# A graph attention kernel with a quantile layer: the first search's transposes one by one, and larger pieces in the quantile sort

## The chip, the cores and the metric

The kernel runs on one core of a Trainium2 chip. The time is the device time of one launch in microseconds. Before the change the median of three runs is 3615.5 us (3614.76 to 3617.49).

## The reference

Two graph layers run one after the other on 4096 nodes of 128 features, with a random adjacency matrix of 0s and 1s (about 32 neighbours a node).

```python
# layer 0: attention over the neighbours, 8 heads
Wh = einsum('nd,hde->hne', nodes, W)
f1 = einsum('hnd,hd->hn', Wh, a1);  f2 = einsum('hnd,hd->hn', Wh, a2)
e = leaky_relu(f1[:, :, None] + f2[:, None, :], 0.2)
att = softmax(where(adj > 0, e, -9e15), axis=-1)
h = elu(einsum('hnm,hmd->hnd', att, Wh))
x1 = layernorm(nodes + elu(concat_heads(h) @ W1 + b1)) * gamma + beta

# layer 1: per feature, three quantiles over the kept neighbours
m = where(num_nbr > 5, ceil(num_nbr / 2), 1)
keep = mask & ~((rank_in_list + 1) % m == 0)
svals = sort(where(keep, x1, big), axis=neighbours)
agg = mean of svals at the places of the 0.25, 0.5 and 0.75 quantile
s = 0.5 * agg + 0.5 * x1
out = s @ W.T + b + x1
```

## The kernel before

The nodes form 32 tiles of 128. The work has four stages.

**First search.** For each node the columns of its neighbours are listed. ScalarE turns half a row tile of the adjacency matrix (128 x 2048 integers) into signs (`sgn`, L642). TensorE multiplies them into keys of 512 columns (two matmuls into the PSUM tile `key`, L681 and L684; `key` has two buffers). VectorE takes the eight largest of each 128 columns (L648), and from those, eight at a time, the list (L653, L655). One step of the generator `neighbours` is one such round: keys of 512 columns for one tile, and one further eight of the list of the tile before. Eight rounds are a tile. After every third tile of the first block, `complete_records` makes the records, in three further steps.

The first block has six tiles, hence 7 x 8 + 2 x 3 = 62 steps. After each of them but the first, the loop at L324 takes one step of the generator `node_rows`. That generator loads W, the attention vectors, the last layer's weights (`wl_sb`) and the node features (`rec`) on ScalarE's DMA queue, folds W and the vectors into `wa` on VectorE, transposes the 32 node tiles on TensorE, copies them out of PSUM on ScalarE (`xT`), multiplies them by `wa`, copies the products (`F`) and stores the rows, features and attention terms, to `xt_d` in HBM on SyncE's queue (L592). In the version before, four transposes make one step and the four products of the previous four another.

**Attention.** The nodes are ranked by their number of neighbours and their records scattered to HBM (GpSimd). Then in blocks of 6, 10 and 16 tiles the neighbours' rows are gathered from `xt_d`, one row for each of 128 partitions a gather (L219), and weighed. The search of the next block runs in between, on VectorE and TensorE.

**Lists of layer 1.** They are made at the end of the last block, with the weights `wt` of the quantile places.

**Quantiles.** Nodes are sorted by length of list. They are handled in 21 units of one tile or of two: unit 0, then the single tiles 24 to 31, then the pairs (22,23) down to (2,3), then tile 1. For a unit of k tiles with n kept neighbours at most, GpSimd gathers n x k rows of `x1` into `vals` (two buffers) and the nodes' own rows into `xs`. VectorE runs a selection network over the n slots, whose steps are elementwise minima and maxima of slots (L1225, between `vals`, two `work` tiles and `goal`). TensorE and ScalarE weigh the results (`st_ps`, L1244), apply the last layer, and GpSimd scatters `o` to the output (L228). GpSimd's queue holds the rows of the next unit ahead of the scatter of the unit before, then the rows of the unit after that. A new unit's `vals` takes the buffer of the unit two before it.

The network's work is issued in pieces: a minimum or maximum of slots that lie at regular distances is one instruction, of c x m x 128 x k columns. The kernel counts how long VectorE has been running since the last turn (`then`, in us, from the constants `TT_FIX`, `TT_EACH`, `TT_OVER`). After more than `TURN_MIN` us it puts in a turn, a copy of one PSUM column (`junk` from `still`, L1196)[...]. A piece that would run beyond `TURN_MAX` is cut so that it ends near `TURN_AIM`.

The order of instructions on TensorE, VectorE, ScalarE and GpSimd is that of the program (`manual_schedule`).

Of the kernel before, what the change touches and what calls it, by code (L numbers as in the profile page):

```python
# [9 lines left out]
F32 = mybir.dt.float32  # L10
# [9 lines left out]
P = 128  # L20
N = 4096
D = 128
H = 8
NT = N // P
# [61 lines left out]


TT_FIX, TT_EACH, TT_OVER = 0.148, 0.001042, 0.077
TURN_MIN, TURN_AIM, TURN_MAX = 1.25, 1.45, 1.7


R_NUM, R_OWN, R_F1 = L, L + 1, L + 2
# [1 line left out]
R_X = R_F1 + H  # L94
# [148 lines left out]
def kernel(  # L243
# [61 lines left out]
    with tc.tile_pool(name="setup", bufs=1) as sp, tc.tile_pool(  # L305
# [15 lines left out]
        )  # L321
        iota(nc, rowi, [[1, P]])
        rows = node_rows(tc, sp, pp, rec, x, W, W_sb, a1, a2, Wl, wa, WlT, ident, bad, xt_d)
        for i, _ in enumerate(search(0, BLOCKS[0])):  # L324
            if i > 0:
# [216 lines left out]
def node_rows(tc, sp, pp, rec, x, W, W_sb, a1, a2, Wl, wa, WlT, ident, bad, xt_d):  # L542


    nc = tc.nc
    c = NT // 4
    load = nc.scalar.dma_start
    load(W_sb, W.rearrange("h d e -> d h e"))
    yield
    a_b = sp.tile([P, 2, H * D], F32, name="a_b")  # L550
    for i, a in enumerate((a1, a2)):
        load(a_b[:, i, :], a.rearrange("h d -> (h d)").partition_broadcast(P))
    wl_sb = sp.tile([P, D], F32, name="wl_sb")
    load(wl_sb, Wl)
    yield
    for i in range(4):
        for _ in range(3):
            yield
        load(
            rec[:, ts(i, c), R_X : R_X + D],  # L560
            x[ts(i, c * P), :].rearrange("(t p) d -> p t d", p=P),
        )
    for i in range(2):
        wprod = sp.tile([P, H, D], F32, name="wprod")
        nc.vector.tensor_tensor(
            wprod, W_sb, a_b[:, i, :].rearrange("p (h d) -> p h d", h=H), ALU.mult
        )
        nc.vector.tensor_reduce(wa[:, ts(i, H)], wprod, AX.X, ALU.add)
        yield
    F = sp.tile([P, NT, 2 * H], F32, name="F")  # L570
    xT = f_ps = None
    for t in range(0, NT + 8, 4):
        if f_ps is not None:
            nc.scalar.copy(F[:, t - 8 : t - 4, :], f_ps)
            f_ps = None
        if xT is not None:
            f_ps = pp.tile([P, 4, 2 * H], F32, name="f_ps")
            for u in range(4):
                nc.tensor.matmul(f_ps[:, u, :], lhsT=xT[:, ts(u, P)], rhs=wa, start=True, stop=True)
            xT = None  # L580
        yield
        if t < NT:
            xt_ps = pp.tile([P, 4 * P], F32, name="xt_ps")
            for u in range(4):
                nc.tensor.transpose(xt_ps[:, ts(u, P)], rec[:, t + u, R_X : R_X + D], ident)
            xT = sp.tile([P, 4 * P], F32, name="xT", bufs=2)
            nc.scalar.copy(xT, xt_ps)
        yield
    for dst, src in ((R_F1, F[:, :, 0:H]), (R_X + D, F[:, :, H:])):
        nc.vector.tensor_scalar(rec[:, :, dst : dst + H], src, FMAX, -FMAX, ALU.min, ALU.max)  # L590
    for i in range(4):
        nc.sync.dma_start(  # L592
            xt_d[ts(i, c * P), :].rearrange("(t p) w -> p t w", p=P),
            rec[:, ts(i, c), R_X:],
        )
    pad = sp.tile([P, XW], F32, name="pad")
    nc.gpsimd.memset(pad[:, 0:D], 0.0)
    nc.gpsimd.memset(pad[:, D:], PADF)
    nc.sync.dma_start(xt_d[N:, :], pad)
    yield  # L600
    sq = sp.tile([P, NT, 2 * H], F32, name="sq")
    nc.vector.tensor_tensor(sq, F, F, ALU.mult)
    fm = sp.tile([P, NT], F32, name="fm")
    nc.vector.tensor_reduce(fm, sq, AX.X, ALU.max)

    nc.vector.tensor_scalar(fm, fm, FMAX * FMAX, None, ALU.is_le)
    nc.vector.tensor_scalar(bad[:, 3, :], fm, -1.0, 1.0, ALU.mult, ALU.add)
    yield
    wl_ps = pp.tile([P, 4 * P], F32, name="xt_ps")[:, 0:D]
    nc.tensor.transpose(wl_ps, wl_sb, ident)  # L610
    nc.scalar.copy(WlT, wl_ps)
# [886 lines left out]
```

## Time and profile before

| | |
|---|---|
| median of three runs | 3615.5 us |
| the profiled execution's own time | 3611.84 us |
| its span, first to last instruction | 3610.1 us |
| first search, first keys to the last list | 8 to 116 us |
| first gather of rows for the attention | 150.8 us |
| first sorting piece of the quantile stage | 1857.3 us |
| last sorting piece | 3596.6 us |
| turns | 1295, 148 ns each |
| sorting pieces | 2649 |

The largest groups of the quantile stage (line, engine, operation, tiles, shapes and count, then busy us and mean ns, then idle time before them):

```profile
L1225 DVE TENSOR_TENSOR work<-work 128x512 f32<-128x512 f32 x507 | 335.9, 682 | 0.1
L1225 DVE TENSOR_TENSOR work<-work 128x1024 f32<-128x1024 f32 x273 | 334.2, 1229 | 0.0
L1196 DVE COPY junk<-still 128x1 f32<-128x1 f32 x1270 | 187.5, 148 | 0.0
L219 POOL DMA_INDIRECT vals<-x_d,idx x970 | 998.3, 1029 | 315.4 <-issue 281.9 <-DVE junk L1196 20.2 <-DMA vals<-x_d,idx 10.4
```

Durations overlap: an instruction of VectorE begins some 0.08 us before the one ahead of it ends, so costs on the engine are read from starts. DVE is VectorE, PE TensorE, ACT ScalarE, POOL GpSimd and SP SyncE. The window of these groups begins at 1900 us, so some counts are below the total.

### The profile page before, as it was taken

The page shows a single profiled execution, that of the slowest core. Times are in us where ns is not written, and L with a number is a line of the kernel's source. Part 1 is how long each engine was busy: PE and PEld are TensorE (multiplying, and loading weights), DVE is VectorE, ACT ScalarE, POOL GpSimd, SP SyncE. Part 2 cuts the span into 40 slices and gives each one's busy share as a digit, 9 for nine tenths or more (in the row PEclk, how much of TensorE's full clock was granted, in tenths as well). Part 3 has the DMA queues.
Part 4 walks back from the last instruction along what each step waited for, and adds up shares of the span by engine and source line. Part 5 has one row for each costly group of instructions (what it writes and reads, how often), then busy time and mean ns, then how long its engine had stood idle before and what let it go on. Part 6 is the DMA issues. An engine that isn't in the chain of part 4 may idle for free. (4 is left out here: it accounts for less than half of the span.)

```text
span 3610.1 us, 22900 instructions
## 1 busy us (share of the span) xinstructions
PE 1258.1 (35%) x5323; PEld 951.4 (26%) x5323; DVE 2742.8 (76%) x7591; ACT 399.5 (11%) x555; POOL 2344.3 (65%) x2341
## 2 busy tenths in 40 slices
PE   6377667878456454456610000000000000001101
PEld 3044545445455454355510000000000000000101
DVE  7787548877345122157448999999999999999998
ACT  3122122322111011111110000000000000000000
POOL 1375767757777777777557776777555766667530
PEclk9965557566556555555555555555555555555555
DMA  6443244432222222222111111111111111111100
GB/s 212 132 147 90 67 149 139 142 123 70 59 63 55 55 55 54 66 58 55 43 38 48 48 47 41 46 47 46 39 34 37 47 44 40 43 45 47 38 20 3
DMA packets 109137, 237.46 MB, mean 66 GB/s; under 512 B 46720, under 2 KB 63104, under 8 KB 100800
## 3 DMA queue, kind: packets, MB, share of 16 engines
q0 software_dynamic: 74368, 156.34, 15.5%
q10 hardware_dynamic: 14848, 70.85, 5.7%
q1 hardware_dynamic: 19776, 8.73, 1.1%
q8 instruction: 44, 0.72, 0.1%
q14 instruction: 101, 0.83, 0.1%
HBM read 224.60 MB, written 11.15 MB: 65 GB/s over the span
## 5 line engine op out<-in xcount | busy, mean ns | idle before, releaser
L219 POOL DMA_INDIRECT G<-xt_d,idx x1124 | 1096.6, 976 | 416.3 <-issue 324.0
L219 POOL DMA_INDIRECT vals<-x_d,idx x1024 | 1052.3, 1028 | 333.9 <-issue 298.0
L1225 DVE TENSOR_TENSOR work<-work 128x512 f32<-128x512 f32 (+6 forms) x1405 | 959.4, 710 | 0.4
L1244 PE MATMUL st_ps<-dg,goal 128*128 128x128 f32 x286 | 71.8, 429 | 1644.7 <-DVE goal L1225 1574.6
L1225 DVE TENSOR_TENSOR work<-work,work 128x512 f32<-128x512 f32 (+5 forms) x958 | 604.9, 655 | 0.7
L1244 PEld LDWEIGHTS st_ps<-dg,goal 128*128 128x128 f32 x286 | 63.8, 324 | 1651.0 <-issue 1650.2
L1012 PE MATMUL y<-wide,G 128*128 128x32 f32 (+3 forms) x2248 | 482.7, 392 | 26.9 <-DVE wide L999 26.9
L1012 PEld LDWEIGHTS y<-wide,G 128*128 128x128 f32 x2248 | 461.2, 309 | 62.3 <-DVE wide L999 30.0
L648 DVE MAX8 first<-key 128x8 f32<-128x128 f32 x1024 | 225.2, 281 | 119.0 <-PE key L684 118.5
L949 DVE TENSOR_TENSOR z<-G,f1x 128x128 f32<-128x128 f32 (+5 forms) x92 | 29.0, 328 | 307.9 <-DMA G<-xt_d,idx 302.7
L228 POOL DMA_INDIRECT out_dram<-o,own_i x32 | 51.0, 1593 | 295.3 <-ACT o L1270 276.1
L681 PE MATMUL key<-sgn,markb 128*128 128x512 bf16 x256 | 149.3, 583 | 145.3 <-DVE first L648 98.2
L1196 DVE COPY junk<-still 128x1 f32<-128x1 f32 x1295 | 191.2, 148 | 0.0
L1225 DVE TENSOR_TENSOR work<-vals 128x1024 f32<-128x1024 f32 (+8 forms) x140 | 138.8, 1007 | 46.2 <-DMA vals<-x_d,idx 45.9
L642 ACT ACTIVATE sgn<-adj_t 128x2048 bf16<-128x2048 int32 x64 | 122.1, 1907 | 355.4 <-PE key L681 304.8
L1043 PE MATMUL small<-W_sb,late 128*128 128x128 f32 x512 | 126.0, 430 | 88.4 <-DVE late L1040 88.4
L1243 ACT ACTIVATE dg<-ident,wt 128x128 f32<-128x128 f32 x143 | 47.5, 393 | 955.9 <-PE st_ps L1244 955.6
L964 PE MATMUL small<-z,own 128*4 128x32 f32 (+6 forms) x438 | 49.6, 280 | 284.8 <-ACT z L956 284.8
L684 PE MATMUL key<-parts,oneb 64*128 64x512 bf16 x256 | 147.2, 575 | 0.2 <-POOL parts L237 0.2
L1043 PEld LDWEIGHTS small<-W_sb,late 128*128 128x128 f32 x512 | 111.7, 324 | 102.7 <-DVE late L1040 99.0
L980 PE MATMUL rz<-rden,ownT 4*128 4x32 f32 (+6 forms) x438 | 97.8, 386 | 78.0 <-DVE rden L975 63.0
L1031 PE MATMUL hT<-late,W_sb 128*128 128x128 f32 x512 | 110.9, 385 | 35.4 <-ACT late L1025 35.4
(184 smaller groups left out, 1763.3 us busy)
## 6 DMA issues: line engine op xcount, KB each, us to landing
adj_t<-in_adj_dram ACTq DMA_DIRECT2D x64, 1024.0 KB
G<-xt_d,idx POOLq DMA_INDIRECT x1124
vals<-x_d,idx POOLq DMA_INDIRECT x1024
R<-rec_d SPq DMA_DIRECT2D x128, 26.2 KB
xt_d<-rec SPq DMA_DIRECT2D x4, 544.0 KB
rec<-in_x_dram ACTq DMA_DIRECT2D x4, 512.0 KB
narrow<-rec_d SPq DMA_DIRECT2D x68, 5.2 KB
a_b<-in_L_gnn_a_dram ACTq DMA_DIRECT2D x2, 512.0 KB
```

Source lines behind the costliest of these rows:

```text
L219: nc.gpsimd.indirect_dma_start(out=dst, out_offset=None, in_=rows, in_offset=bass.IndirectOffsetOnAxis(ap=idx, axis=0),)
L642: nc.scalar.activation(sgn, adj_t, AF.Sign, accum_out=cnt[:, i : i + 1])
L648: nc.vector.max(first[:, ts(c0 // CW + c, 8)], key[:, ts(c, CW)])
L681: nc.tensor.matmul(key, lhsT=markb, rhs=sgn[:, ts(b, 512)], start=True, stop=False)
L684: nc.tensor.matmul(key, lhsT=oneb[0:64, :], rhs=parts[1][:, ts(r - 1, 512)] if r else parts[0], start=False, stop=True)
L980: nc.tensor.matmul(rz[:, layer[i] * H : (layer[i] + w - g0) * H], lhsT=ownT[w][:, r, :], rhs=rden.rearrange("p (g r h) -> p r g h", r=k // ...
L1012: nc.tensor.matmul(yf[:, ts(g, c)], lhsT=G[:, col + j - a, 0:D], rhs=pf[:, ts(j, c)], start=(i == 0 and g % (w // 2) == w // 2 - 1), stop= ...
L1031: nc.tensor.matmul(hT[:, ts(h, P)], lhsT=consts["W_sb"][:, h, :], rhs=yT[:, h, :], start=True, stop=True)
L1043: nc.tensor.matmul(o, lhsT=hv[:, h, :], rhs=consts["W1_sb"][:, h, :], start=(h == 0), stop=(h == H - 1))
L1196: nc.vector.tensor_copy(junk, late["still"])
L1225: nc.vector.tensor_tensor(slots_of(dst, (j, c, s, m), size), slots_of(a, (i, c, s, m), size), slots_of(b, (i + d, c, s, m), size), op,)
L1244: nc.tensor.matmul(st_ps[:, u, :], lhsT=goal[:, (j * k + u) * D : (j * k + u + 1) * D], rhs=dg, start=(j == 0), stop=False,)
```

## The change

Three things are changed.

1. The quantile stage's limits: a turn after more than 1.1 us (before 1.25), pieces cut to end near 1.9 us (before 1.45), and only if they would run beyond 2.4 us (before 1.7). A piece of 2048 columns stays whole.
2. In `node_rows`, one transpose and one product go behind each round, the product three tiles behind its transpose; the copy `xT` is of one tile, in five buffers, and each four products are copied to `F` one step after the last of them.
3. The loads of W, the vectors and the last layer's weights start four rounds later and the next two further on; the node features follow two rounds apart instead of three.

```diff
-TURN_MIN, TURN_AIM, TURN_MAX = 1.25, 1.45, 1.7
+TURN_MIN, TURN_AIM, TURN_MAX = 1.1, 1.9, 2.4
...
     load = nc.scalar.dma_start
+    for _ in range(4):
+        yield
     load(W_sb, W.rearrange("h d e -> d h e"))
-    yield
+    for _ in range(2):
+        yield
     a_b = sp.tile([P, 2, H * D], F32, name="a_b")
...
     for i in range(4):
-        for _ in range(3):
+        for _ in range(2):
             yield
...
-    xT = f_ps = None
-    for t in range(0, NT + 8, 4):
-        if f_ps is not None:
-            nc.scalar.copy(F[:, t - 8 : t - 4, :], f_ps)
-            f_ps = None
-        if xT is not None:
-            f_ps = pp.tile([P, 4, 2 * H], F32, name="f_ps")
-            for u in range(4):
-                nc.tensor.matmul(f_ps[:, u, :], lhsT=xT[:, ts(u, P)], rhs=wa, start=True, stop=True)
-            xT = None
+
+    LAG = 3
+    turned, f_ps = [], None
+    for t in range(NT + LAG):
+        if t < NT:
+            xt_ps = pp.tile([P, 4 * P], F32, name="xt_ps")[:, 0:P]
+            nc.tensor.transpose(xt_ps, rec[:, t, R_X : R_X + D], ident)
+            xT = sp.tile([P, P], F32, name="xT", bufs=LAG + 2)
+            nc.scalar.copy(xT, xt_ps)
+            turned.append(xT)
+        u = t - LAG
+        if u >= 0:
+            if u % 4 == 0:
+                f_ps = pp.tile([P, 4, 2 * H], F32, name="f_ps")
+            nc.tensor.matmul(f_ps[:, u % 4, :], lhsT=turned.pop(0), rhs=wa, start=True, stop=True)
         yield
-        if t < NT:
-            xt_ps = pp.tile([P, 4 * P], F32, name="xt_ps")
-            for u in range(4):
-                nc.tensor.transpose(xt_ps[:, ts(u, P)], rec[:, t + u, R_X : R_X + D], ident)
-            xT = sp.tile([P, 4 * P], F32, name="xT", bufs=2)
-            nc.scalar.copy(xT, xt_ps)
-        yield
+        if u > 0 and u % 4 == 3:
+            nc.scalar.copy(F[:, u - 3 : u + 1, :], f_ps)
```

## The prediction

> **What bounds the kernel now.** I read the page first (busy shares, slices), then busy time by stretch, then the timelines of single engines where a stretch was not clear.
>
> ```profile
> PE 1258.1 (35%) x5323; PEld 951.4 (26%) x5323; DVE 2742.8 (76%) x7591; ACT 399.5 (11%) x555; POOL 2344.3 (65%) x2341
> DVE  7787548877345122157448999999999999999998
> POOL 1375767757777777777557776777555766667530
> L228 POOL DMA_INDIRECT out_dram<-o,own_i x32 | 51.0, 1593 | 295.3 <-ACT o L1270 276.1
> ```
>
> No engine bounds the whole span. From slice 21 on VectorE is at 9 in every slice, while GpSimd, which issues the gathers, sits 276 us waiting for the result `o` of a unit whose sort has not ended. So the quantile stage is VectorE's. Before it, GpSimd stands at 7 tenths over long stretches, and that is full: a gather takes 0.94 us, and the next begins 0.30 us after it.
>
> ```profile
> 24.67:44.00 19.33, 11.15 (x20) 1.95 (x19) 18.95 (x69) 5.70 (x6) 0.83 (x3) 1.00 1.05 354
> 44.00:80.00 36.00, 35.27 (x123) 22.22 (x123) 27.27 (x118) 12.79 (x22) 0.00 (x0) 1.00 0.27 88
> 1857.30:3596.60 1739.30, 122.00 (x528) 104.84 (x529) 1723.92 (x3944) 56.56 (x177) 1114.61 (x1064) 0.52 0.14 40
> ```
>
> The columns are window, length, then busy time and count of PE, weight loads, DVE, ACT, POOL. The quantile stage is 1739.3 us long and VectorE idles 15 us of it (13.9 at its start, where the second unit's gathers are awaited). In the first search VectorE is full from 24.67 to 44 and then, with the transposes, loses 36.00 - 27.27 = 8.7 us to a TensorE that is full.
>
> ```profile
> 50.81 1.89 PE L579 MATMUL f_ps<-wa,xT 128*128 128x16 f32 x8
> 52.53 0.59 PE L681 MATMUL key<-sgn,markb 128*128 128x512 bf16 x1
> 53.59 1.12 PE L585 MATMUL xt_ps<-ident,rec 128*128 128x128 f32 x4
> 54.50 0.63 PE L681 MATMUL key<-sgn,markb 128*128 128x512 bf16 x1
> 53.70 0.89 DVE L648 MAX8 first<-key 128x8 f32<-128x128 f32 x4 [1.14 <-PE key L684]
> 24.67 0.89 DVE L648 MAX8 first<-key 128x8 f32<-128x128 f32 x4 [4.81 <-PE key L684]
> 150.82 0.98 POOL L219 DMA_INDIRECT G<-xt_d,idx  x1 [5.63 <-issue]
> ```
>
> Starts give the cost in the queue: four products 1.72 us (50.81 to 52.53), two key products 1.06, four transposes 0.91.
>
> ```profile
> 2109.24 0.95 DVE L1225 TENSOR_TENSOR work<-work,vals 128x768 f32<-128x768 f32 x1
> 2110.11 0.15 DVE L1196 COPY junk<-still 128x1 f32<-128x1 f32 x1
> 2110.18 1.48 DVE L1225 TENSOR_TENSOR work<-vals 128x1280 f32<-128x1280 f32 x1
> 2111.57 0.15 DVE L1196 COPY junk<-still 128x1 f32<-128x1 f32 x1
> 2109.43 1.57 POOL L219 DMA_INDIRECT vals<-x_d,idx  x1 [0.30 <-issue]
> 2111.31 1.17 POOL L219 DMA_INDIRECT vals<-x_d,idx  x1 [0.30 <-issue]
> ```
>
> This is the rule of the stage. The gather begun at 2109.43 ends at 2111.00, 0.89 after the turn at 2110.11; that of 2111.31 ends at 2112.48, 0.91 after the turn at 2111.57. A gather waits for the next start of a VectorE instruction and ends 0.90 later. By the timeline it is let in between two sorting pieces too, with no turn between (about 90 of 100 such cases). A turn costs VectorE 0.069 us (2110.11 to 2110.18), not its 0.15.
>
> [...] Here, from starts, a piece of n columns takes 0.0685 + n/960 us (512: 0.602; 1024: 1.135), so the fixed part is 0.0685.
>
> **The change, part by part.**
>
> *Quantile pieces and turns.* The instruction orders of the two builds, counted: pieces 2649 before, 2250 after; turns 1295 and 1118; the columns handled are the same, 1,382,784. Fewer pieces: 399 x 0.0685 = 27.3 us. Fewer turns: 177 x 0.069 = 12.2 us. All of it lies on VectorE, which is the path: 39.5 us.
>
> Collisions: all pieces and turns of before at these prices make 1711.3 us, yet the stage less its 13.9 us wait took 1725.4, so 14 us are lost otherwise. A part shows: 305 pieces of 1024 columns behind a turn that let a gather in took 1.159 on average instead of 1.132, 8 us. There the gather falls due just as the turn runs, since 1.20 us of piece and turn nearly match the gather's 1.245. With longer pieces the gather is waiting already, and 768-column pieces show no such loss at the median. I take 9 us for after, so 5 gained (bounds 0 and 12).
>
> Gathers get slower. Does a stall come in? The nearest to it is the run of pairs (18,19) to (6,7). After the change they hold 59, 59, 55, 56, 50, 51, 51 turns in sorts of 94.0, 94.0, 88.4, 88.8, 79.3, 80.9, 80.9 us (606 by the prices above), 1.59 us to a turn, against 1.26 before. One gather to a turn is then 1.6 us. By the timeline of before, when the sort of (18,19) begins (2790), the rows of (16,17) are in. From there to the sort of (4,5) GpSimd must issue the rows of six pairs, 62+62+58+58+58+54 = 352, and 12 scatters of results: 364 x 1.6 = 582, plus 9 between paired scatters (1.5 each), and it can't start before `o` of (20,21) is there, 8 us in: 599 of 606 us, with some 3 us of collisions on VectorE's side. So it just holds, with 10 us to spare of the 87 by which the last rows of (4,5) are early now, and GpSimd's waits of 1.6 to 28.6 us for `o` there vanish. In (22,23) and (20,21), at 1.44 to a turn, 70 operations take 101 of 112 us, and it is level at their end. The second unit's rows, awaited at the start, come perhaps 1 us later. Sum of the stage: 39.5 + 5 - 1 = 43 us (bounds 20 and 52).
>
> *First search, TensorE.* It removes eight groups of four transposes and four products in turn, and adds one of each to 35 rounds. A round's own VectorE work is 1.58 us (starts at 102.26 and 103.84). Before, two rounds took TensorE 4.79 (50.81 to 55.60) against 3.16. After, one round takes 1.06 to 1.10 + 0.91/4 + 1.72/4 = 1.74, and 1.80 if a lone transpose costs 0.27 and a lone product 0.45, as the first of each group does. Some 26 rounds hold both beside keys (three of the 35 fall in the record completion, three at each end hold one only): 26 x 0.16 to 0.22 = 4 to 6 us idle where 8.7 stood. Gain 4; bounds -5 [...] and +8. ScalarE has 32 copies of 128 columns for 8 of 512, in a queue with the 2.1 us signs; a transpose waits only for the copy two rounds (3.3 us) back, so this is hidden.
>
> *First search, loads.* `W_sb`, `a_b` and `wl_sb`, 1.6 MB on ScalarE's queue, go behind one more sign and the adjacency load after it. Now they are issued at 17 to 21 while VectorE waits 4.81 us for an adjacency tile with the DMA at 0.9: up to 2.5 us gained. They are needed by the weight products, which stand two rounds later; if they land late, up to 3 us lost. I take 0. The node loads come closer together, each needed later than now.
>
> *The store of `xt_d`* moves from step 36 to step 52 of 62, from 86.4 to about 107 us. Its four DMAs stand on SyncE's queue ahead of the record reads at 144. 2.2 MB at the 200 to 318 GB/s of that stretch are 7 to 11 us: in by 120, and the first gather, at 150.8 now, waits for records, not for it. Hidden by ranking and the record scatters (to 142); beyond that each us counts fully. The clip and the bounds on F move with it on VectorE, same count.
>
> Between the first search and the sort the built orders of PE, DVE and ACT are the same, those of POOL and SP throughout. GpSimd runs full from the first gather, so 4 us earlier there is taken as 4 us at the end. At the end nothing changes: the last scatter stands about 5 us behind the last piece.
>
> **Sum.** 43 + 4 = 47 us. Against the profiled execution's 3611.8 us (span 3610.1 and 1.7 around it): 3565. The median of the runs is 3.7 above it: 3615.5 - 47 = 3568.5, so 3569.
>
> **Rivals.**
> 1. *GpSimd late in the last pairs.* At 1.68 us an operation instead of 1.6 the 364 need 29 us more; 10 are covered, VectorE waits about 19: 3588. For it: the margin is 2%, and no piece over 1408 columns ran before. Against: gathers that waited for 1280 columns kept to the 0.90, and some will be let in between pieces inside a run.
> 2. *The first search turns worse*, -5 instead of +4 by lone weight loads, and 3 by late loads: 3581. Against: in the groups the switch from bf16 keys to fp32 cost at most 0.06 us.
> 3. *GpSimd becomes the bound, and it is slower than before.* Mechanism: [...] behind a 1536 or 2048-column piece (1.67 or 2.20 us) it misses two openings. It decides where 364 operations eat the 10 us and the 47 gained: 1.6 + 57/364 = 1.76 us each. At 2.0, a longer run each time: 364 x 0.4 - 10 = 136 lost, 3705. Against: gathers now end in the midst of the piece behind the opening, so one was enough.
> That the change doesn't do what it says is excluded by the counts.
>
> **Chances.** Forecast 0.70, rival 1 0.13, rival 2 0.07, rival 3 0.10. Range: 3556 (collisions nearly gone, +8 in the search) to 3592 (rival 1 at its worse), which leaves rival 3 out and a little at each end. A measurement tells 0.2% (7 us) from no change. Faster 0.87 (the first three, less 0.03), same 0.03, slower 0.10.
>
> **What would show it.** Copies of `still` 1118 at 0.15; a stage from first piece to last of about 1696 us; VectorE still at 9 to the end and idle for `vals` only at the start; gathers' mean up from 1.03 to near 1.2 and GpSimd's wait for `o` far below 276 us; VectorE idle for keys in the search 4 to 6 us; the first gather near 147. Wrong: VectorE waiting for `vals` in the pairs below (14,15), pieces of 2048 columns costing more than 2.2 us, or a first gather after 151.

## The result, and the profile after

The changed kernel takes 3559.96 us (median of four runs, 3557.06 to 3561.82), the kernel before, run beside it, 3615.13 us (3607.5 to 3617.49). The ratio is 0.985, with a 95% interval of 0.9833 to 0.9867: 55 us less. The two profiled executions have spans of 3560.0 and 3610.1 us, 50.1 apart, and the readings below divide these 50. The other 5 us of the medians lie in the scatter of the runs: the profiled execution of before is 3.3 us below the median beside it, that of after 1.8 above.

The page of the changed kernel (lines below the change stand 3 further down: the sorting piece is L1228, the turn L1199; the transposes are L580, their products L588):

```profile
PE 1257.6 (35%) x5323; PEld 949.8 (27%) x5323; DVE 2700.2 (76%) x7015; ACT 403.2 (11%) x579; POOL 2510.0 (71%) x2341
...
DVE  8787458877435222247538999999999999999998
...
POOL 1475767657777777777747777788777688777771
...
L219 POOL DMA_INDIRECT vals<-x_d,idx x1024 | 1219.8, 1191 | 315.7 <-issue 308.7
...
L1199 DVE COPY junk<-still 128x1 f32<-128x1 f32 x1118 | 168.8, 151 | 0.0
...
L228 POOL DMA_INDIRECT out_dram<-o,own_i x32 | 44.7, 1398 | 105.9 <-ACT o L1273 83.6
```

VectorE is still at 9 to the end. GpSimd is busy 71% of the span instead of 65%: a gather of the quantile stage takes 1.191 us on average instead of 1.028, and GpSimd's wait for a finished unit (`o`) has shrunk from 276.1 to 83.6 us.

Busy time by stretch (window, length, then PE, weight loads, DVE, ACT, POOL):

```profile
20.20:44.00 23.80, 15.26 (x29) 3.10 (x29) 23.31 (x88) 8.44 (x10) 0.83 (x3) 1.00 1.02 349
44.00:80.00 36.00, 31.83 (x103) 15.48 (x103) 34.76 (x156) 14.01 (x35) 0.00 (x0) 1.00 0.44 147
1847.20:3546.60 1699.40, 120.90 (x528) 103.81 (x529) 1681.92 (x3368) 56.57 (x177) 1282.30 (x1064) 0.52 0.16 41
```

- The quantile stage, from first to last piece, takes 1699.4 us instead of 1739.3: 39.9 less.
- In the stretch of the transposes VectorE idles 36.00 - 34.76 = 1.2 us instead of 8.7. The first gather of the attention begins at 137.69 instead of 150.82: 13.1 earlier.
- From the first gather to the first sorting piece it is 1709.5 us instead of 1706.5. These two make the sort begin at 1847.2 instead of 1857.3: 10.1 earlier.

13.1 - 3.0 + 39.9 = 50.0. The 3.0 is no effect that can be named: in the five profiled executions whose first search is the changed one, on chips as fast as this (this one, e5, e6, e7 and e12), that part took 1705.3 to 1709.6 us.

VectorE's waits in the first 120 us, before and after:

```profile
DVE first L648 <- PE key L684: 14.0, 18, 4.8
```

```profile
DVE first L651 <- PE key L687: 1.8, 7, 0.5
```

Of the 12.2 us gone, 4.5 are one wait: the round that began at 24.67 after 4.81 us begins at 20.21 after 0.35. The loads of the weights no longer stand beside that adjacency tile (W is issued at 19.39, not 17.18); e4 below changes the loads alone. Most of the rest is the 8.7 us that became 1.2.

TensorE and VectorE in the timeline of the changed kernel, one round and the start of the next:

```profile
52.52 0.48 PE L580 MATMUL xt_ps<-ident,rec 128*128 128x128 f32 x1
52.53 0.61 PEld L588 LDWEIGHTS f_ps<-wa,xT 128*128 128x128 f32 x2
52.80 0.45 PE L588 MATMUL f_ps<-wa,xT 128*128 128x16 f32 x2
...
53.08 0.59 PE L684 MATMUL key<-sgn,markb 128*128 128x512 bf16 x1
...
53.46 0.88 DVE L651 MAX8 first<-key 128x8 f32<-128x128 f32 x4
53.60 0.10 PEld L687 LDWEIGHTS <-oneb 64*128 64x128 bf16 x1 [0.44 <-issue]
53.60 0.60 PE L687 MATMUL key<-parts,oneb 64*128 64x512 bf16 x1
54.14 0.18 PEld L580 LDWEIGHTS xt_ps<-ident,rec 128*128 128x128 f32 x1 [0.44 <-issue]
54.14 0.47 PE L580 MATMUL xt_ps<-ident,rec 128*128 128x128 f32 x1
...
54.69 0.59 PE L684 MATMUL key<-sgn,markb 128*128 128x512 bf16 x1
...
55.06 0.88 DVE L651 MAX8 first<-key 128x8 f32<-128x128 f32 x4
```

From starts: keys 53.08 to 54.14, 1.06 us; transpose 52.52 to 52.80 and product 52.80 to 53.08, 0.28 each. A round is 1.61 us on TensorE (53.08 to 54.69) and 1.60 on VectorE (53.46 to 55.06). The product's two passes start at 52.80 and 52.87, the keys at 53.08. Its first weights start loading at 52.53, beside the transpose; its first pass costs 0.07 us and its second 0.21. In the groups of four before, eight passes end to end took 1.72 us, 0.215 a pass and 0.43 a product.

The two largest pieces in the sort, with GpSimd:

```profile
2802.41 2.29 DVE L1228 TENSOR_TENSOR work<-work 128x2048 f32<-128x2048 f32 x1
2803.61 1.90 POOL L219 DMA_INDIRECT vals<-x_d,idx  x1 [0.30 <-issue]
2804.61 0.15 DVE L1199 COPY junk<-still 128x1 f32<-128x1 f32 x1
...
2805.88 2.28 DVE L1228 TENSOR_TENSOR work<-work 128x2048 f32<-128x2048 f32 x1
2807.07 1.91 POOL L219 DMA_INDIRECT vals<-x_d,idx  x1 [0.30 <-issue]
2808.08 0.15 DVE L1199 COPY junk<-still 128x1 f32<-128x1 f32 x1
2808.15 1.21 DVE L1228 TENSOR_TENSOR work<-work 128x1024 f32<-128x1024 f32 x1
```

A piece of 2048 columns takes 2.20 us by starts (2802.41 to 2804.61). The gather begun at 2803.61 ends at 2805.51, 0.90 after the turn at 2804.61; that of 2807.07 ends at 2808.98, 0.90 after the turn at 2808.08. Of 643 gathers of rows that had begun more than 0.06 us before a turn and still stood there, 642 were let in by it, that is, ended within 1.0 us of its start.

The number to watch is the margin: from the end of a unit's last gather to its first piece. For the pairs (18,19), (16,17) and so on to (4,5) it was 139, 121, 107, 100, 95, 86, 80, 87 us and is 115, 104, 80, 62, 55, 41, 23, 14. For (4,5), the last gather and the first piece, before and after:

```profile
3334.02 1.10 POOL L219 DMA_INDIRECT vals<-x_d,idx  x1 [0.31 <-issue]
3422.33 1.22 DVE L1225 TENSOR_TENSOR work<-vals 128x1024 f32<-128x1024 f32 x1
```

```profile
3359.64 1.23 POOL L219 DMA_INDIRECT vals<-x_d,idx  x1 [0.30 <-issue]
3374.80 1.75 DVE L1228 TENSOR_TENSOR work<-vals 128x1536 f32<-128x1536 f32 x1
```

### The profile page after: what moved, and what is told of

The parts are those of the page before. It is cut to its first block, busy times and chain, and to the rows that moved or that the text cites. A ratio compares the mean times of both kernels' runs of the same rounds, so it can differ in the third digit from the quotient of the medians.

```text
span 3560.0 us, 22296 instructions
## 1 busy us (share of the span) xinstructions
PE 1257.6 (35%) x5323; PEld 949.8 (27%) x5323; DVE 2700.2 (76%) x7015; ACT 403.2 (11%) x579; POOL 2510.0 (71%) x2341
## 5 line engine op out<-in xcount | busy, mean ns | idle before, releaser
L219 POOL DMA_INDIRECT vals<-x_d,idx x1024 | 1219.8, 1191 | 315.7 <-issue 308.7
L1228 DVE TENSOR_TENSOR work<-work 128x512 f32<-128x512 f32 (+7 forms) x1194 | 933.7, 811 | 0.6
L1228 DVE TENSOR_TENSOR work<-work,work 128x512 f32<-128x512 f32 (+6 forms) x821 | 590.8, 741 | 0.5
L1228 DVE TENSOR_TENSOR work<-vals 128x1536 f32<-128x1536 f32 (+7 forms) x96 | 133.4, 1404 | 47.9 <-DMA vals<-x_d,idx 47.5
L1199 DVE COPY junk<-still 128x1 f32<-128x1 f32 x1118 | 168.8, 151 | 0.0
L228 POOL DMA_INDIRECT out_dram<-o,own_i x32 | 44.7, 1398 | 105.9 <-ACT o L1273 83.6
```

Source lines behind the costliest of these rows:

```text
L219: nc.gpsimd.indirect_dma_start(out=dst, out_offset=None, in_=rows, in_offset=bass.IndirectOffsetOnAxis(ap=idx, axis=0),)
L1199: nc.vector.tensor_copy(junk, late["still"])
L1228: nc.vector.tensor_tensor(slots_of(dst, (j, c, s, m), size), slots_of(a, (i, c, s, m), size), slots_of(b, (i + d, c, s, m), size), op,)
```

## The experiments

Theory: the gain is two separate parts. VectorE's own work in the sort falls, and GpSimd just keeps up; the first search loses the idle time of VectorE. The rivals are that GpSimd becomes the bound, or that one part holds only through the other. Eight of the twelve runs came from two chips on which the kernel before takes 4587 (first four) and 4573 us (e8 to e11). A reading from those is used only for a part that takes the same time there; the rest stands under e8 to e11.

**The two parts, and the two halves of the search's part (e1 to e4).**

```diff
# e1: the kernel before, with
+TURN_MIN, TURN_AIM, TURN_MAX = 1.1, 1.9, 2.4
# e2: the changed kernel, with
+TURN_MIN, TURN_AIM, TURN_MAX = 1.25, 1.45, 1.7
# e3: e2, the loads where they were before
-    for _ in range(4):
-        yield
     load(W_sb, W.rearrange("h d e -> d h e"))
-    for _ in range(2):
-        yield
+    yield
...
-        for _ in range(2):
+        for _ in range(3):
             yield
# e4: e2, four transposes and four products in turn as before
-    for t in range(NT + LAG):
+    for t in range(0, NT + 8, 4):
...
```

> The kernel before with the three new turn limits alone (1.1, 1.9, 2.4); the first search as before. Theory: the two halves of the change add up, and the limits are worth what the sort stage shows, about 40 us: stage from first to last sorting piece 1699 us (1739 before), VectorE idle for vals only before the second unit, first gather still at 150.8 us, time about 3615 - 40 = 3575 us. Rival: the sort gained from the earlier start of the stage (other DMA traffic, other alignment of gathers), so that alone the limits give clearly less, stage above 1710 us.

> The kernel after with the old turn limits (1.25, 1.45, 1.7): only the first search is changed. Theory: VectorE's wait for keys falls from 14.0 to about 1.8 us, the first gather comes at 137.7 us, and the 13 us are carried to the end but for a few: stage of the sort 1739 us, beginning at 1845 to 1848, time 3615 - 10 to 13 = about 3603. Rival: the attention blocks take the gain back (they wait for something else), then the sort begins within 3 us of 1857 and the time stays within 4 us of 3615.

> The kernel before with one transpose and one product behind each round, but the loads of W and the vectors where they were (one and one step, three between the node loads), old limits. Theory: the 4.8 us wait of VectorE for the second adjacency tile (at about 20 us) is due to those loads and comes back, the waits for keys between 44 and 80 us stay away: key waits 6 to 7 us, first gather at about 142 to 143 us. Rival: the interleaving did everything, and the tile's wait was not due to the loads: first gather at 138.

> The kernel before with only the later loads (four steps, then two, two between the node loads); four transposes and four products in turn as before, old limits. Theory: the early wait for the adjacency tile is gone (0.4 instead of 4.8 us), the waits for keys beside the groups of transposes stay (some 9 us): first gather at about 146 us. Rival: the loads move the wait elsewhere (the products of the weights wait for W), first gather at 150 or later.

The first gather, which these chips start as the other does: e1 150.3, e2 138.6, e3 141.1, e4 146.7 us. e1 has the search of before on the same chip. Against its 150.3, the tiles one by one (e3) bring 9.2 us and the later loads (e4) 3.6; both together (e2) bring 11.7 here, and 13.1 in the changed kernel against 150.8. So the halves add up to within about 1 us, and the larger is that of the single transposes. VectorE's waits for keys in the first 120 us show the same: 13.0 us in e1 (the longest 3.8), 5.3 in e3 (3.9), 9.6 in e4 (1.4) and 2.9 in e2 (1.5). The times of the whole kernel (e1 4349.5, ratio 0.9519, 0.9421 to 0.9617; e2 4571.0, ratio 0.9986, 0.996 to 1.0012; e3 4555.9 and e4 4598.2, one run each) missed what was expected: the limits brought 237 us between the medians, not 40, and the search nothing that could be measured (10 us would be 0.2%, which lies inside the interval of e2).

**Are the turns needed (e5, e6)?** Both leave out the copies; the counting and cutting stay, e6 with the old limits.

```diff
-        nc.vector.tensor_copy(junk, late["still"])
+        return
# e6 also
+TURN_MIN, TURN_AIM, TURN_MAX = 1.25, 1.45, 1.7
```

> The kernel after (limits 1.1, 1.9, 2.4) without the turns' copies: the pieces are the same 2250. The output is the same. Theory: a gather is let in at the start of any VectorE instruction, a turn is only one more start. VectorE's own work falls by 1118 x 0.069 = 77 us to 1595, but GpSimd, which has 14 us to spare with turns, now has fewer starts and less time: VectorE waits for vals in the last pairs, some 50 us, stage about 1690 to 1710, time 3550 to 3572, same or a little better. Rival: only a turn lets GpSimd in; between two pieces with no wait it stays locked out. Then gathers take many us each and the stage is far above 2000 us.

> The kernel after with the old limits (1.25, 1.45, 1.7) and without the turns' copies: the pieces are the 2649 of before, none over 1408 columns. Theory (any start lets a gather in): VectorE's own work is 1711 - 1295 x 0.069 = 1622 us, a start comes every 1.5 us at the latest, so GpSimd keeps up with 38 us or more to spare; stage 1636 to 1685 with the 14 us at its start and collisions, time about 3500 to 3546: faster than the kernel after. Rival (only turns let GpSimd in): stage far above 2000 us.

e5 took 3648.3 us, ratio 1.0104 (1.0088 to 1.0121): slower than the kernel before, though VectorE has 77 us less to do than in the changed kernel. Its stage is 1789.1 us, well above the 1690 to 1710 expected. Its page, and VectorE's waits in it:

```profile
DVE  8777368777253122266459999999999877877888
```

```profile
DVE work L1228 <- DMA vals<-x_d,idx: 189.5, 13, 32.1
```

The 9s end at the pair (16,17): from its start to that of the next, each unit from (16,17) to (4,5) takes 21.1 to 24.9 us more than its pieces cost by the prices, 159 in sum. There GpSimd is the bound. A gather takes 1.335 us on average, and 1004 of the 1024 take 3 us or less. One of the other 20, in the timeline of e5:

```profile
2515.33 13.81 POOL L219 DMA_INDIRECT vals<-x_d,idx  x1 [0.30 <-issue]
```

```profile
2515.14 0.88 DVE L1228 TENSOR_TENSOR goal<-work,work 128x128 f32<-128x128 f32 x4
2515.95 0.48 DVE L1228 TENSOR_TENSOR goal<-work 128x128 f32<-128x128 f32 x2
...
2518.57 4.01 DVE L1228 TENSOR_TENSOR work<-vals 128x1024 f32<-128x1024 f32 x3
...
2528.36 1.23 DVE L1228 TENSOR_TENSOR work<-work,work 128x1024 f32<-128x1024 f32 x1
```

That gather ended at 2529.14 only, with some twenty starts of pieces in between. In the changed kernel no gather took over 3 us. What shuts a gather out in such a stretch isn't known.

e6 took 3553.7 us, ratio 0.9844 (0.9828 to 0.9861), which can't be told from the changed kernel. Its stage, 1696.2 us, is longer than expected: VectorE's work is 1621.9 at the fixed prices, but (6,7), (4,5) and (2,3) take 12.4, 14.3 and 9.3 us more than that, 32.2 of these 36 us in waits for rows. So gathers get through without turns too; but 642 of 643 that stood at a turn ended within 1.0 us of it, while without turns one stood for 13.8 us in e5 and one for 13.5 in e6, and in both runs the last pairs wait.

**Is the bound on pieces needed (e7)?** No piece is cut, up to 4096 columns.

```diff
-TURN_MIN, TURN_AIM, TURN_MAX = 1.1, 1.9, 2.4
+TURN_MIN, TURN_AIM, TURN_MAX = 1.1, 1.9, 99.0
```

> The kernel after with no piece cut (limits 1.1, 1.9, 99): 2191 pieces, the largest of 4096 columns (4.3 us), 1061 turns. VectorE's own work falls by 8 us to 1664. Theory: the change stands at the edge, GpSimd had 14 us to spare at (4,5), and these longer pieces use it up: VectorE waits for vals in the pairs from (10,11) on, some 25 us besides the 15 at the start; stage about 1710, slower than the 1699 of after. Rival: GpSimd is let in often enough whatever the length; no wait for vals in the pairs, stage about 1690.

3586.0 us in a single run, its stage 1727.7. VectorE's own work is 8 us less than in the changed kernel, but the margin is down to 5 us at (10,11), and VectorE then waits 13.9, 12.9 and 8.0 us for the rows of (8,9), (6,7) and (4,5), each of which it begins within 2 us of the unit's last gather:

```profile
DVE work L1228 <- DMA vals<-x_d,idx: 34.8, 3, 13.9
```

The 14 us left by a bound of 2.4 are all there is: the rival of late rows becomes true one step further on.

**The parts again, and turns only where GpSimd needs them (e8 to e11).** e8 is e1 again and e9 is e2. In e10, units of a single tile, before which GpSimd is well ahead, get no turns and the old limits; in e11 the pairs (22,23) and (20,21) too.

```diff
+    bare = k == 1              # e11: k == 1 or n >= 34
+    t_min, t_aim, t_max = (1.25, 1.45, 1.7) if bare else (TURN_MIN, TURN_AIM, TURN_MAX)
...
-        nc.vector.tensor_copy(junk, late["still"])
+        if not bare:
+            nc.vector.tensor_copy(junk, late["still"])
```

> The kernel before with the new limits of pieces and turns alone (1.1, 1.9, 2.4), the first search as before. If the gain is the sum of two separate parts, the first gather stays at 150.8 us, the quantile stage takes the 1699 us that it takes in the changed kernel, and the time is about 40 us below the kernel before: ratio 0.989. Rival, an earlier start is needed for the stage to hold: then GpSimd's margin before the last pairs is gone and the stage takes over 1710 us, ratio above 0.992.

> The changed kernel with the old limits (1.25, 1.45, 1.7): the first search and its loads alone. Theory: first gather at 137.7 us, sort begun at 1847, stage 1739 us as before, so about 10 us below the kernel before: ratio 0.997. Rival, the 13 us at the first gather are lost again in the attention, where GpSimd isn't the bound everywhere: the sort begins after 1853 and the ratio is above 0.9985.

> The changed kernel, but the units of a single tile (where GpSimd is 14 to 100 us ahead) have the old limits and no turns; the pairs are as in the changed kernel. VectorE's own work falls by 21.8 us (by the fixed prices of pieces and turns). Theory: the margin at the pair (4,5) is set by the pairs themselves from (22,23) on and stays near 14 us, so the whole of it is gained: stage 1676 to 1685 us, time 3538 to 3545 us. Rival: without turns a gather is locked out for up to 13.5 us among short pieces, the singles' lead shrinks by 20 us or more, and VectorE waits for rows in the pairs after all: 3555 us or more.

> As the previous one, with the pairs (22,23) and (20,21) without turns too: VectorE's own work 29.5 us below the changed kernel's. Theory: the margin at (18,19) falls by what these two pairs no longer take, about 8 us plus what slower gathers cost, and the 14 us at (4,5) just cover it: waits of 0 to 10 us, 3533 to 3548 us. Rival: gathers behind these pairs are late by over 20 us, and the waits for rows in the pairs from (6,7) on take more than was saved: 3555 us or more.

They ran on another of the slow chips:

| run | us | ratio to before | 95% interval |
|---|---|---|---|
| e8 | 4338.7 | 0.9491 | 0.9443 to 0.9539 |
| e9 | 4565.5 | 0.9991 | 0.9968 to 1.0015 |
| e10 | 4341.4 | 0.951 | 0.9459 to 0.956 |
| e11 | 4352.4 | 0.9531 | 0.9481 to 0.958 |

The expected times are missed in all four. Most of what these chips take longer stands before the sort: from first gather to sort 2396 us in e8 (1706.5 in the kernel before on the fast chip), and why isn't known. The sort takes 1799.1 us in e8 and 2042.0 in e9. VectorE's waits in e9 from 2900 us on:

```profile
DVE junk L1199 <- remote: 101.9, 38, 3.6
DVE junk L1199 <- DVE work L1228: 64.9, 56, 1.5
DVE junk L1199 <- issue: 34.6, 17, 3.5
```

The turns themselves come late there, mostly with no releaser that the trace shows. In e8, which has fewer, the same lines sum to 19.3 us (11.7, 4.0 and 3.6). From the start of (22,23) to that of (4,5) the sort took 1085.1 us in e9 and 835.2 in e8, where it took 863.4 in the kernel before and 835.3 in the changed one on the fast chip. So with the new limits these pairs run as fast as there, and most of what the limits gain on the slow chips is that the late turns are gone (201.4 us of these waits in e9, 19.3 in e8, where the sort is 242.9 us shorter). The granted TensorE clock is the same on all chips (0.56), so it isn't that. Why turns come late with the old limits, and hardly with the new, stays open.

What can be read is the margin. From (22,23) on, e8's pairs run as in the changed kernel, with margins of 122, 104, 80, 62, 55, 42, 25, 15 us from (18,19) to (4,5) and no wait over 1 us, although its first search is the old one: the sort holds without the earlier start. In e11 the margin at (4,5) is -8 us (the last gather ends within the sort) and VectorE waits 7.6 us there (7 us of margin and no wait in e10): what two pairs without turns took of the margin is missing at the end of the row of pairs.

The mixture gains nothing here: e10 and e8 have overlapping intervals, though e10 has the changed search too. Up to the start of (22,23) its sort takes 800.7 us against 792.2, since pieces begin late there where turns did: the waits of VectorE before pieces of `work` with no releaser shown sum to 101.5 us, against 30.6 in e8. One gather for (20,21) stood, in e10 and in e11, through 144 starts of pieces of a single tile without turns:

```profile
3181.44 85.74 POOL L219 DMA_INDIRECT vals<-x_d,idx  x1 [11.57 <-DVE work L1231]
```

After it the margin at (18,19) is 91 us in e10, where it is 122 in e8. No pair of e10 had to wait for that, but half of the margin at (4,5) is gone.

**The mixture on a chip like the first (e12).** The kernel of e10.

> The changed kernel, with the single-tile units without turns and at the old limits, once more. In the run before, its margin before (4,5) was 7 us and no pair waited for rows, while the pair (18,19) began with 91 us of margin instead of 115. Theory: VectorE's own work is 21.8 us below the changed kernel's and no wait comes in, so the stage takes 1676 to 1684 us and the time, where the kernel before takes about 3611, is 3538 to 3546: ratio 0.980. Rival: lock-outs among the singles' short pieces cost 15 us or more at their own starts: stage above 1690, ratio 0.984 or more, no better than the changed kernel.

3541.5 us (3537.5 to 3543.3), before 3613.6; ratio 0.9796 (0.978 to 0.9813), an interval wholly below that of the change. The page of e12:

```profile
DVE  8786558877435221247538999999999999999998
...
L219 POOL DMA_INDIRECT vals<-x_d,idx x1024 | 1196.6, 1169 | 314.2 <-issue 306.3
...
L228 POOL DMA_INDIRECT out_dram<-o,own_i x32 | 57.4, 1795 | 103.9 <-ACT o L1276 81.6
```

VectorE at 9 to the end, GpSimd's wait for `o` as in the changed kernel, and the margins at (18,19) and (4,5) the same as there, 115 and 14 us. The stage is 1684.1 us, at the edge of what was expected: of the 21.8 us saved, 15.3 arrive, since 6.4 are lost among the single tiles (some 2 of it at the second unit's rows). The sort also began 3.1 us earlier, which lies within the scatter given above. This is the fastest version that ran on the fast chips; on the slow one the same kernel, e10, kept only 7 us of margin and was no faster than e8. Why the gather of 85.7 us has no like in e12 isn't known.

## Why the prediction was right, and where it was off

- **Pieces and turns (39.5 us).** Right. At the prices read from starts, 0.0685 + n/960 a piece and 0.069 a turn, VectorE's work falls from 1711.2 to 1671.7 us. The stage fell by 39.9.
- **Collisions (5 us).** Mis-sized: what the stage takes beyond those prices and the first wait fell from 14.1 to 11.9 us, 2.2. **The second unit's rows (1 us later):** 14.0 to 15.8, 1.8 later. Sum of the stage 39.9 by these terms instead of 43.
- **GpSimd just holds, with 10 us to spare.** Right, and this was the term with the most at stake: 87 us of margin at (4,5) became 13.9. The operation of 1.6 us is measured at 1.53 to 1.60 from (14,15) to (4,5). e7 shows that the margin was the limit: with longer pieces (8,9), (6,7) and (4,5) wait. The rule behind it, that a gather is let in by the next start of a VectorE instruction, holds for turns (642 of 643 within 1.0 us); e5 shows starts of pieces that don't let it in (13.81 us, through some twenty).
- **TensorE's round in the first search.** The step that failed: 1.74 to 1.80 us were taken and 1.61 measured. The term is the lone product, priced at 0.43 to 0.45 from the groups of four, where it costs 0.28: the weights of its first pass load beside the transpose ahead of it (from 52.53), and that pass takes 0.07. So 1.2 us of idle remain, not 4 to 6. e3 puts this half at 9.2 us at the first gather, where 4 were forecast.
- **Later loads (0).** Mis-sized: the wait of 4.81 us was gained almost whole, 4.5 in the trace and 3.6 in e4, outside the bound of 2.5. That bound took the tile to gain only a part of the wait; with the 1.6 MB issued later 0.35 us of the wait were left.
- **The store of `xt_d`.** Issued at 97 us, not 107, and hidden: the first gather came earlier, not later.
- **The sum.** 40 from the stage and 10 from the search stand where 43 and 4 were forecast: 50 against 47. That the two lie so close is in part luck: two errors of opposite sign, 3 too many and 6 too few.
- **The rivals.** Rival 1 didn't occur, but e7 makes it by longer pieces. Rival 2 went the other way; its -5 was the author's estimate. Rival 3's premise, that behind a long piece a gather misses two openings, is refuted by the lines at 2803.61 and 2807.07: behind 2048 columns it ends 0.90 us after the start of the next turn, so one is enough. Its outcome, GpSimd as the bound and a kernel slower than before, is real in e5 (3648.3 us), where gathers stood through starts of pieces. What holds a gather back while VectorE works was not shown by any run.

Not measured on a fast chip: each of the two parts alone. That they add up there rests on the accounts of the two traces, on the first gathers of e1 to e4, e8 (150.3) and e9 (137.9), and on the margins of e8.

## What to carry to other kernels

Price a single instruction from its place in the queue, not from the mean of a group of its kind: here the first weight load of the lone product lay beside the transpose ahead of it, and the product took 0.28 us instead of 0.43. Where one engine is full and the gathers of another stand until one of its instructions starts (here 642 of 643 ended within 1.0 us of a turn's start), watch how far the second is ahead unit by unit: shorten the first one's work as long as that margin is positive, and drop the openings only where it doesn't fall to nothing later. That margin is not the same on every chip: the kernel of e10 and e12 kept 7 us on one and 14 on the other. A load that isn't needed yet can cost a wait elsewhere: moving 1.6 MB of it took 3.6 to 4.5 us from the wait for an adjacency tile.

## What the runs showed of the hardware that was not expected

- A lone fp32 product of 16 columns behind a transpose took 0.28 us of TensorE, against 0.43 in a row of four.
- Without turns, in e5, 1004 of 1024 gathers took 3 us or less, but one stood through some twenty starts of pieces, 13.8 us. The like occurs in e6 at the same place (13.5 us), in e12 at another (13.9), and in e10 and e11 for 85.7 us. With the turns of the changed kernel the longest gather took 2.8 us.
- On two chips the kernel before took 27% longer at the same granted clock (0.56). Most of it stands before the sort: from first gather to sort 2396 us in e8, which up to there is the kernel before, against 1706.5 on the fast chip. With the old limits turns began late there (201.4 us of waits in e9 from 2900 us on), 136.5 of it with no releaser that the trace shows; the limits were worth about 5% there (0.9519 in e1, 0.9491 in e8), and by the stage about 1% on the fast chip (39.9 us).
